# Moving statistics, the last addition of a convolution and unit orders in a fused graph-attention kernel

## The chip, the cores and the metric

One core of one Trainium2 chip runs the whole program; seven cores stand idle. The metric is the time of one execution in microseconds on the device. The engines of the core work side by side, each through its own queue in order: TensorE (PE in the profile; its weight loads are PEld), VectorE (DVE), ScalarE (ACT), GpSimd (POOL), and SyncE (SP), which issues the DMAs here. An instruction starts when what it waits for on other engines is done and everything ahead of it in its own queue has been issued.

## What is computed

Two layers for each of 32 batches of a 512 x 512 block x, in float32. The adjacency matrix adj is 512 x 512, of zeros and ones, shared by all batches.

```python
def attention(x, adj, Wq, bq, Wk, bk, Wv, bv):        # 8 heads of 64
    q, k, v = x @ Wq + bq, x @ Wk + bk, x @ Wv + bv   # split into heads
    scores = q @ k.T / sqrt(64) + where(adj == 0, -1e9, 0)
    return softmax(scores) @ v

def convolution(x, adj, W, b):
    return (adj @ x) @ W + b

x = layernorm(x + attention(x, adj, ...))     # first normalisation, "which" 0
x = layernorm(x + convolution(x, adj, W1, b1))  # second, "which" 1
```

## The kernel before

The fast path, `fast_kernel`, is followed by a general one that runs only when a check on the data fails (here it does not run). A batch's rows x lie in `X[b]` as four blocks of 128 rows (index c). A product of 512 x 512 x 512 is made by Strassen's scheme in Winograd's form: seven products of 256 x 256 x 256 (`FACTORS`, in the order 1, 5, 6, 7, 2, 3, 4), each of eight matmul records of 256 columns in the profile (L367), whose results VectorE, ScalarE and GpSimd add up. The left factors need three or four sums of blocks, which GpSimd makes (`combine_rows`, L329 to L331, and `sum_rows`, L357); the factors of q, k and v come from x transposed (`turn_squares`, L351).

Names for what follows, each with its lines:

- `project` (L367, evicted in L389 to L402): product i of q, k or v.
- `scores(b, g)` (L563 to L567): eight heads are taken in two groups g of four, each of two pairs hp. Sixteen score tiles of 128 x 512 go through eight PSUM banks (`bank`, a ring of 8, shared by all results of TensorE). VectorE empties each bank while masking it (L565), and ScalarE makes exponentials (L567) in the tiles `e`, of which there are 8. GpSimd adds the exponentials of a pair over the four blocks (`add_exponentials`, L578, into `es`).
- `attend` (L587): values times exponentials; the result is copied by ScalarE to `attT` (L591), of which there are two tiles. It also allots the tile `SQUARES`, one of the `e` tiles, for the fold.
- `fold_squares` (L598, L600): VectorE transposes and sums `es` of a pair; `add_up` (L608 to L613) finishes the softmax's sums and inverts them.
- `residual` (L619 to L624): TensorE turns `attT` over, VectorE multiplies by the inverse and adds to `X[b]`. After the last pair of a batch it issues the four `statistics` of the first normalisation (L429, L430: mean and variance of one block).
- `norm` (L433 to L445): a square root on ScalarE, its inverse and the shift on VectorE, four normalisations on ScalarE. `survey` gives the four statistics of the second normalisation.
- `split_high`, `split_low` (L455, L459, L460): x as a sum of two parts that the fast matmul format holds exactly; GpSimd adds the convolution's bias b1 to x after. `aggregate` (L486 to L492): adj times x, quarter d at a time.
- `convolve(b, i)` (L525 to L539): product i of the convolution. Its results go straight into the quarters x11, x12, x21, x22 of `X[b]`; a helper tile `MIX` collects the parts that several quarters share. Product 6 adds to MIX, and GpSimd adds MIX to x12; product 7 adds to MIX again, and GpSimd adds MIX to x22 and x21 (L537). Products 3 and 4 are then added to x12 and x21 by VectorE (L539).
- `look_for_low_half` (L306 to L309), once for each block of adj: does the fast format hold it exactly? ScalarE makes a copy, VectorE compares it (into a tile `attT`) and counts.

The order is written out by hand. `units_of(b)` makes the list of units that fill TensorE's time between the attentions of batch b: projections of batch b + 1, the split, aggregation and convolution of batch b - 1, the transposes of batch b + 2 and the normalisations. `behind[k]` is what is issued behind the k-th of the first 16 projection units. `weighed` gives each unit a weight (0.5 for a project or convolve, 0.55 for an aggregate, none for most), and `work_until(part)` issues units until that part of the group's weight is done. For each group the loop issues: two `attend`, the two folds, the next group's `scores`, `add_up`, units up to 0.85 (group 0) or 0.6 (group 1; 1.0 in the last batch but one, B - 2), the residuals, the rest of the units. `release()` issues the `add_exponentials` of the second pair, held back until a projection i = 7 has been issued (until any convolve in the last batch).

In the steady loop a batch therefore runs: attend(b, 0), folds, scores(b, 1), q, k and the first of v of batch b + 1 with the residual of group 0 among them; attend(b, 1), folds, scores(b + 1, 0), the rest of v, aggregation of b - 1, residual of group 1, statistics, convolution of b - 1. The last batch, t = B - 1 = 31, has no projections left; its list `units` holds the low halves of batch 30 (`lows`), the convolution of batch 29 (`older`), the aggregation of batch 30 (`gathered`) and the survey. After the loop come the convolution of batch 30, batch 31's normalisation by rows (`split_rows`, L500, L501; `aggregate_rows`, L513 to L523), its convolution, and a last normalisation by half blocks (`half_statistics`, L793).

## Time and profile before

| what | us |
|---|---|
| median of 3 runs | 2858.62 |
| lowest, highest | 2857.77, 2861.34 |
| profiled execution, span | 2858.2 |
| TensorE busy | 2820.5 |
| VectorE busy | 2086.4 |
| GpSimd busy | 1746.2 |
| ScalarE busy | 1146.6 |
| steady batch, start to start (1025.22 to 1113.04) | 87.82 |
| of which TensorE busy | 87.74 |

Busy time of an engine is the time in which the profile shows an instruction on it; ends of matmuls are modelled, so a wait between two matmuls of a pipelined run can be hidden in it. Times in the timelines are microseconds from the span's start. An entry in square brackets at the end of a timeline line is the time for which that engine stood idle before the instruction, and who ended it. The chain of waits is followed back from the last instruction to what released each step. A matmul of the program appears as two records or more, so counts of records are multiples of the program's.

### The profile page before, as it was taken

The numbers are of one execution on the slowest core, as the hardware profiler recorded it, in microseconds if no ns is written. First come the engines' busy times: TensorE is split into PE (matmuls) and PEld (weight loads), VectorE is DVE, ScalarE is ACT, GpSimd is POOL, SyncE is SP. The second block draws the span as 40 slices with busy tenths as digits, with TensorE's granted clock in tenths as the row PEclk, the third lists the DMA queues.
The fourth block names the chain that finished last, engine by engine and source line by source line (L and its number), as shares of the span: only waits on it lengthen the run. The fifth ranks groups of instructions, "written<-read, shape, count | busy, mean of one in ns | idle before, by whom it ended". The sixth has DMA issues, their size and how long they took to land.

```text
span 2858.2 us, 35612 instructions
## 1 busy us (share of the span) xinstructions
PE 2820.5 (99%) x13346; PEld 1983.1 (69%) x13346; DVE 2086.4 (73%) x3415; ACT 1146.6 (40%) x1550; POOL 1746.2 (61%) x1096
## 2 busy tenths in 40 slices
PE   8999999999999999999999999999999999999997
PEld 6676776766767767667677676676676766766765
DVE  6767777677776777777777767777677777777786
ACT  3344343343433443434434334343344342443443
POOL 4565665665756656656566656575665665665763
PEclk9999999999999999999999999999999999999998
DMA  5001111111101111011111111110111111111001
GB/s 154 12 8 41 45 30 30 41 34 45 45 16 45 34 41 45 16 45 34 41 45 35 25 42 33 45 45 15 45 34 41 45 24 36 36 39 45 30 16 45
DMA packets 302577, 108.81 MB, mean 38 GB/s; under 512 B 264256, under 2 KB 268352, under 8 KB 302400
## 3 DMA queue, kind: packets, MB, share of 16 engines
q1 hardware_dynamic: 302400, 106.47, 14.6%
q8 instruction: 108, 1.77, 0.3%
q14 instruction: 69, 0.57, 0.1%
HBM read 72.88 MB, written 33.55 MB: 37 GB/s over the span
## 4 chain that ended last, share of the span: by engine, by line
PE 96%; DVE 2%; POOL 1%; SPq 0%; issue 0%; ACT 0%; DMA 0%; DVEq 0%; ACTq 0%; POOLq 0%
PE bank L367 53%; PE bank L563 17%; PE bank L587 15%; PE bank L486 8%; PE bank L619 2%; PE bank L608 0%; POOL es L578 0%; DVE bnst L429 0%; SPq L253 0%; DMA xin<-in_x_dram 0%; DVE e L598 0%; POOL xs L460 0%; DVE bank L622 0%; POOL xs L537 0%; DVE part L600 0%
## 5 line engine op out<-in xcount | busy, mean ns | idle before, releaser
L565 DVE SCALAR_TENSOR_TENSOR e<-gap,bank 128x512 f32<-128x512 uint8 x1024 | 617.4, 678 | 65.0 <-PE bank L563 65.0
L578 POOL TENSOR_TENSOR es<-e 128x1024 f32<-128x1024 f32 x128 | 316.2, 2470 | 530.5 <-ACT e L567 530.5
L578 POOL TENSOR_TENSOR es<-es,e 128x1024 f32<-128x1024 f32 x256 | 618.7, 2417 | 20.1
L567 ACT ACTIVATE e<-e 128x1024 f32<-128x1024 f32 x512 | 524.2, 1052 | 130.8 <-DVE e L565 103.0
L591 ACT ACTIVATE attT<-bank 128x512 f32<-128x512 f32 x128 | 76.4, 598 | 1046.7 <-PE bank L587 1046.7
L563 PE MATMUL bank<-q,k 64*128 64x512 f32 x2048 | 488.4, 603 | 2.4 <-ACT attT L591 2.4
L587 PE MATMUL bank<-e,v 128*64 128x512 f32 x2048 | 453.8, 595 | 1.9 <-DVE v L402 1.9
L367 PE MATMUL bank<-wv,xT 128*128 128x256 f32 x1792 | 411.5, 381 | 3.1 <-DVE q L402 3.1
L563 PEld LDWEIGHTS bank<-q,k 64*128 64x128 f32 x2048 | 223.7, 186 | 265.6 <-issue 161.2
L367 PE MATMUL bank<-xT,wk 128*128 128x256 f32 x1792 | 404.0, 380 | 0.7 <-DVE wk L317 0.7
L367 PE MATMUL bank<-xT,wq 128*128 128x256 f32 x1792 | 401.0, 381 | 2.5 <-DVE wq L317 1.8
L367 PE MATMUL bank<-w,yT 128*128 128x256 f32 x1792 | 394.0, 380 | 1.6 <-DVE yT L518 1.6
L367 PEld LDWEIGHTS bank<-xT,wk 128*128 128x128 f32 x1792 | 341.1, 190 | 47.6 <-PE bank L367 1.1
L367 PEld LDWEIGHTS bank<-w,yT 128*128 128x128 f32 x1792 | 339.2, 191 | 47.2 <-DVE yT L518 2.0
L367 PEld LDWEIGHTS bank<-xT,wq 128*128 128x128 f32 x1792 | 337.7, 190 | 49.2 <-POOL xT L331 1.8
L367 PEld LDWEIGHTS bank<-wv,xT 128*128 128x128 f32 x1792 | 335.3, 190 | 49.3 <-issue 3.4
L587 PEld LDWEIGHTS bank<-e,v 128*64 128x64 f32 x2048 | 141.6, 137 | 278.8 <-issue 268.2
L537 POOL TENSOR_TENSOR xs<-xs,mix 128x512 f32<-128x512 f32 x93 | 117.6, 1279 | 204.2 <-DVE mix L535 204.2
L460 POOL TENSOR_TENSOR xs<-xs,b_r 128x512 f32<-128x512 f32 x124 | 157.2, 1278 | 114.4 <-DVE low L459 114.4
L402 DVE TENSOR_TENSOR q<-bank,q 128x512 f32<-128x512 f32 x96 | 66.4, 691 | 183.0 <-PE bank L367 157.2
L444 ACT ACTIVATE xs<-xs,shift,rstd 128x512 f32<-128x512 f32 x248 | 184.8, 811 | 29.8 <-DVE shift L439 29.8
L489 ACT ACTIVATE yT<-bank 128x512 f32<-128x512 f32 x124 | 74.3, 599 | 294.9 <-PE bank L486 294.9
(115 smaller groups left out, 3016.7 us busy)
## 6 DMA issues: line engine op xcount, KB each, us to landing
xin<-in_x_dram SPq DMA_DIRECT2D x496, 64.0 KB, 2.3
xs<-in_x_dram SPq DMA_DIRECT2D x31, 1024.0 KB, 5.1
out_dram<-xs SPq DMA_DIRECT2D x31, 1024.0 KB, 4.3
xin<-in_x_dram SPq DMA_DIRECT2D x4, 256.0 KB, 3.6
wq<-in_L_gnn_Wq_dram SPq DMA_DIRECT2D x2, 512.0 KB, 6.5
wk<-in_L_gnn_Wk_dram SPq DMA_DIRECT2D x2, 512.0 KB, 8.2
yT<-in_adj_dram SPq DMA_DIRECT2D x1, 1024.0 KB, 7.8
wv<-in_L_gnn_Wv_dram SPq DMA_DIRECT2D x2, 512.0 KB, 8.8
```

Of the source, the lines that this page charges most:

```text
L367: nc.tensor.matmul(pm[:, r, :], left[:, d, r * P:(r + 1) * P], right[:, d, :], start=(d == 0), stop=(d == 1))
L444: nc.scalar.activation(row, row, AF.Identity, bias=SHIFT[t][:, slot:slot + 1], scale=RSTD[t][:, slot:slot + 1])
L460: nc.gpsimd.tensor_add(cols, cols, b1_r[:, None, d * P:(d + 1) * P].to_broadcast([P, NB, P]))
L486: nc.tensor.matmul(pm.rearrange("p a n -> p (a n)"), part, adjT[:, n % NB, :], start=(n == 0), stop=(n == 2 * NB - 1))
L489: nc.scalar.activation(yt[:, d // 2:d // 2 + 3:2, d % 2, :], pm, AF.Copy)
L537: nc.gpsimd.tensor_add(block, block, MIX[b])
L563: nc.tensor.matmul(ps[s], keys[:, j * P:(j + 1) * P], queries, start=True, stop=True)
L565: nc.vector.scalar_tensor_tensor(e[:, s, :], gap[:, j, :], NEG * root, ps[s], op0=ALU.mult, op1=ALU.add)
L567: nc.scalar.activation(e, e, AF.Exp, scale=1.0 / root)
L578: nc.gpsimd.tensor_add(ES[b, hp], ES[b, hp] if j > 1 else E[b, hp, 0], E[b, hp, j])
L587: nc.tensor.matmul(po[s * HD:(s + 1) * HD, :], values, e[:, s, :], start=(j == 0), stop=(j == NB - 1))
L591: nc.scalar.activation(AT[b, hp], po, AF.Copy)
```

## The change

It has these parts:

1. In `convolve`, for all batches but the last, GpSimd adds MIX to x22 only behind product 7; it adds MIX to x21 after VectorE has added product 4 to x21 (a new line behind L539). In the last batch the order of the two is x21, x22 in place of x22, x21. The sums of the next factors (`turned[4:]`, that is `sum_rows`) are issued behind the seventh product of the convolution in place of the fifth.
2. The four statistics of the first normalisation are no longer issued by `residual`, but as units `fresh` among the q projections of the next batch (two each behind the fourth and fifth projection; all four behind the first in batch 1). Batch 30 keeps them in `residual`. The square root and inverse, made for both normalisations at once before (`both`, eight columns), become two of four columns each.
3. `look_for_low_half` moves in batch 0 from behind the projections of q and k to between those of v, two before and two after the residual.
4. In batch 30 `work_until` stops at 0.6 in place of 1.0 ahead of the residual of group 1.
5. In batch 31 two of the low halves of batch 30 are issued between the folds of group 0, and the last group's two folds are issued among the units (`last`), their results in a tile `v` in place of an `e` tile. `release()` is called before the second of these.
6. At the end, the survey of batch 30 is issued whole behind the first product of batch 31's convolution, not half of it before the aggregation; the half statistics of blocks 0 and 1 are taken behind product 3 alone, those of blocks 2 and 3 behind product 4.

```diff
@@ -533,10 +533,13 @@
             nc.scalar.activation(MIX[b], pm, AF.Copy)
         if i in (6, 7):
             nc.vector.tensor_add(MIX[b], pm, MIX[b])
-            for block in (x12,) if i == 6 else (x22, x21):
+            for block in (x12,) if i == 6 else (x21, x22) if b == B - 1 else (x22,):
                 nc.gpsimd.tensor_add(block, block, MIX[b])
         for block in {1: (x11,), 5: (x12, x22), 2: (x11,), 3: (x12,), 4: (x21,)}.get(i, ()):
             nc.vector.tensor_add(block, pm, block)
+        if i == 4 and b < B - 1:
+
+            nc.gpsimd.tensor_add(x21, x21, MIX[b])
 
     def aggregation(b):
 
@@ -586,7 +589,8 @@
                 values = V[b][hp // 2][:, j, h * HD:(h + 1) * HD]
                 nc.tensor.matmul(po[s * HD:(s + 1) * HD, :], values, e[:, s, :],
                                  start=(j == 0), stop=(j == NB - 1))
-        SQUARES[b, hp] = work.tile([P, 2, N], FP, name="e", bufs=8)
+        if (b, hp // PAIRS) != (B - 1, HP // PAIRS - 1):
+            SQUARES[b, hp] = work.tile([P, 2, N], FP, name="e", bufs=8)
         AT[b, hp] = work.tile([P, N], FP, name="attT")
         nc.scalar.activation(AT[b, hp], po, AF.Copy)
 
@@ -594,7 +598,11 @@
 
         if hp % PAIRS == 0:
             PART[b, hp // PAIRS] = work.tile([P, GROUP, N // SQ], FP, name="part", bufs=1)
-        square = SQUARES.pop((b, hp))
+        if (b, hp // PAIRS) == (B - 1, HP // PAIRS - 1):
+
+            square = work.tile([P, 2, N], FP, name="v", bufs=3)
+        else:
+            square = SQUARES.pop((b, hp))
         nc.vector.transpose(square.rearrange("p s n -> p (s n)"), ES.pop((b, hp)).rearrange("p s n -> p (s n)"))
         heads = slice(2 * (hp % PAIRS), 2 * (hp % PAIRS) + 2)
         nc.vector.tensor_reduce(PART[b, hp // PAIRS][:, heads, :], square.rearrange("p s (j f) -> p s j f", f=SQ),
@@ -622,7 +630,7 @@
         nc.vector.tensor_mul(pt, pt, inverse[:, :, :, None].to_broadcast([P, NB, 2, HD]))
         cols = X[b][:, :, hp * P:(hp + 1) * P]
         nc.vector.tensor_add(cols, pt.rearrange("p c s d -> p c (s d)"), cols)
-        if hp == HP - 1 and b < B - 1:
+        if hp == HP - 1 and b == B - 2:
             for c in range(NB):
                 statistics(b, 0, c)
 
@@ -689,16 +697,18 @@
 
             older = convolution(b - 2)
             lows = [(split_low, b - 1, d) for d in range(DB - 1)]
-            units = weighed(lows[:2] + older[:3] + lows[2:] + splits[3:] + older[3:5] + older[5:] + gathered + seen)
+            last = folds(b, 1)
+            units = weighed(older[:3] + last[:1] + lows[2:] + splits[3:] + older[3:] + gathered + last[1:] + seen)
             return units, [sum(w for _, w in units)] * 2
 
+        fresh = [(statistics, b - 1, 0, c) for c in range(NB)] if young else []
         if old:
-            both = [[(f, b - 1, slice(0, 2 * NB))] for f in (square_root, invert_root)]
-            behind = [seen[:2], seen[2:]] + both + [old[2:4], old[4:] + ready] + [[u] for u in young[2:]]
+            behind = [seen[:2], seen[2:], old[:2], old[2:4] + fresh[:2], old[4:] + ready + fresh[2:]] + [
+                [u] for u in young]
         else:
-            behind = [ready] + [[u] for u in young]
+            behind = [ready + fresh] + [[u] for u in young]
         if b == 0:
-            behind = [[]] + [[(sum_weights, w1, n)] for n in range(4)] + [[(look_for_low_half, c)] for c in range(NB)]
+            behind = [[]] + [[(sum_weights, w1, n)] for n in range(4)]
         behind += [[] for _ in range(11 - len(behind))] + [splits[:1], [], splits[1:2]]
         behind += [[] for _ in range(16 - len(behind))]
         units = []
@@ -706,13 +716,14 @@
             units += [unit] + behind[k]
         first = sum(w for _, w in weighed(units))
         values = made[16:]
-        units += values[:3] + gathered[:1] + splits[2:3] + gathered[1:2] + values[3:] + splits[3:]
+        looked = [(look_for_low_half, c) for c in range(NB)] if b == 0 else []
+        units += values[:3] + looked[:2] + gathered[:1] + splits[2:3] + gathered[1:2] + values[3:] + looked[2:] + splits[3:]
         if b == B - 2 > 0:
             units += [(load, B - 1)]
         units += gathered[2:3] + turned[:1] + gathered[3:]
         convolved = convolution(b - 1) if b < B - 2 else []
         for k in range(7):
-            units += convolved[k:k + 1] + (turned[k + 1:k + 2] if k < 3 else turned[4:] if k == 4 else [])
+            units += convolved[k:k + 1] + (turned[k + 1:k + 2] if k < 3 else turned[4:] if k == 6 else [])
         units = weighed(units)
         return units, [first, sum(w for _, w in units)]
 
@@ -733,6 +744,8 @@
             begin = ends[g - 1] if g else 0.0
             while units and (units[0][1] == 0 or done < begin + (ends[g] - begin) * part - 0.3):
                 unit, w = units.pop(0)
+                if unit[0] == fold_squares and unit[2] % PAIRS:
+                    release()
                 run([unit])
                 done += w
                 if unit[0] == (project if b < B - 1 else convolve):
@@ -741,17 +754,17 @@
 
         for hp in range(g * PAIRS, (g + 1) * PAIRS):
             attend(b, hp)
-        folded = folds(b, g)
         if i == len(groups) - 1:
-            run(folded)
             add_up(b, g)
             break
-        run(folded[:1] + flips(1) + folded[1:] if i == 0 else folded)
+        between = flips(1) if i == 0 else [(split_low, b - 1, d) for d in range(2)] if i == len(groups) - 2 else []
+        folded = folds(b, g)
+        run(folded[:1] + between + folded[1:])
         later = scores(*groups[i + 1])
         add_up(b, g)
         if g == 0 and b + 2 < B:
             load_squares(b + 2)
-        work_until((0.6 if b != B - 2 else 1.0) if g else 0.85)
+        work_until(0.6 if g else 0.85)
         for hp in range(g * PAIRS, (g + 1) * PAIRS):
             residual(b, hp)
         work_until(1.0)
@@ -780,7 +793,6 @@
     run(rest[3 + NB:])
     for c in range(NB):
         add_bias(t, c)
-    run(seen[:2])
     aggregate_rows(t)
 
 
@@ -793,14 +805,14 @@
         nc.vector.bn_stats(halves[c][:, s, :], X[t][:, c, s * half:(s + 1) * half])
 
     old = norm(t, 1)
-    beside = {1: seen[2:], 2: old[:2], 5: old[2:3], 6: old[3:5], 7: old[5:]}
+    beside = {1: seen, 2: old[:2], 5: old[2:3], 6: old[3:5], 7: old[5:]}
     for unit in last:
         run([unit] + beside.get(unit[2], []))
         if unit[2] == 2:
             well = judge()
         if unit[2] == 7 and t > 0:
             store(t - 1)
-        for c, s in {2: ((0, 0), (1, 0)), 3: ((2, 1), (3, 1), (0, 1), (1, 1)), 4: ((2, 0), (3, 0))}.get(unit[2], ()):
+        for c, s in {2: ((0, 0), (1, 0)), 3: ((0, 1), (1, 1)), 4: ((2, 1), (3, 1), (2, 0), (3, 0))}.get(unit[2], ()):
             half_statistics(c, s)
             if (c < 2) == (s == 1):
                 if t + 1 not in STAT:
```

## The prediction

> **What bounds the kernel now.** First the page: busy time, then the chain of waits by engine.
>
> ```profile
> PE 2820.5 (99%) x13346; PEld 1983.1 (69%) x13346; DVE 2086.4 (73%) x3415; ACT 1146.6 (40%) x1550; POOL 1746.2 (61%) x1096
> ...
> PE 96%; DVE 2%; POOL 1%; SPq 0%; issue 0%; ACT 0%; DMA 0%; DVEq 0%; ACTq 0%; POOLq 0%
> ```
>
> TensorE sets the time, and the 1% in which it is idle (37.7 us) is small. So I looked inside its busy time: TensorE's timeline, for pieces of one kind that last longer than their like. Columns: start us, length us, engine, line, operation, tiles, shape, count, then the wait.
>
> ```profile
> 99.12 2.68 PE L367 MATMUL bank<-wv,xT 128*128 128x256 f32 x8 [3.15 <-DVE q L402]
> ...
> 139.30 7.69 PE L563 MATMUL bank<-q,k 64*128 64x512 f32 x32
> ...
> 1060.94 7.21 PE L563 MATMUL bank<-q,k 64*128 64x512 f32 x32
> ...
> 1085.64 12.25 PE L367 MATMUL bank<-w,yT 128*128 128x256 f32 x56
> 1097.83 7.09 PE L587 MATMUL bank<-e,v 128*64 128x512 f32 x32
> 1104.84 8.07 PE L563 MATMUL bank<-q,k 64*128 64x512 f32 x32
> ...
> 2766.48 5.56 PE L563 MATMUL bank<-q,k 64*128 64x512 f32 x20 [2.36 <-ACT attT L591]
> ...
> 2793.91 3.41 PE L486 MATMUL bank<-adjT,k 128*128 128x512 f32 x8 [2.93 <-DVE mix L535]
> ...
> 2808.63 0.31 PE L608 MATMUL bank<-part,fold 128*32 128x16 f32 x8 [4.29 <-DVE part L600]
> ...
> 2834.27 11.92 PE L367 MATMUL bank<-w,yT 128*128 128x256 f32 x54 [1.65 <-DVE yT L518]
> ```
>
> Scores (L563) take 7.21 us after a projection, but 8.07 after the convolution and attend (1085.64, 1097.83): 0.86 us more, with no wait shown. The chain of waits has that longer piece (8.00 or 8.01) once in each of 29 batches, every 87.8 us from 226.8 to 2685.6. VectorE's timeline shows why:
>
> ```profile
> 95.64 0.69 DVE L308 TENSOR_TENSOR attT<-yT,high 128x512 f32<-128x512 f32 x1 [13.03 <-PE bank L619]
> ...
> 140.95 9.64 DVE L565 SCALAR_TENSOR_TENSOR e<-gap,bank 128x512 f32<-128x512 uint8 x16
> ...
> 1062.10 9.65 DVE L565 SCALAR_TENSOR_TENSOR e<-gap,bank 128x512 f32<-128x512 uint8 x16 [2.15 <-PE bank L563]
> ...
> 1098.14 0.69 DVE L535 TENSOR_TENSOR mix<-bank,mix 128x512 f32<-128x512 f32 x1 [1.38 <-POOL xs L537]
> 1098.75 0.68 DVE L539 TENSOR_TENSOR xs<-bank,xs 128x512 f32<-128x512 f32 x1
> 1101.46 0.69 DVE L539 TENSOR_TENSOR xs<-bank,xs 128x512 f32<-128x512 f32 x1 [2.03 <-POOL xs L537]
> ...
> 1106.88 9.64 DVE L565 SCALAR_TENSOR_TENSOR e<-gap,bank 128x512 f32<-128x512 uint8 x16
> ```
>
> L565 empties the score banks. Where VectorE waits for it (1062.10, 1.16 us after the scores began at 1060.94) TensorE loses nothing. Where L565 comes behind a backlog TensorE runs out of banks: begun 2.04 us after the scores, the loss is 0.86; 1.65 us after (140.95 against 139.30), 7.69 - 7.21 = 0.48. So loss = lateness - 1.17, which I use throughout.
>
> **What the skill says.** "Trainium Kernel Development and Optimization", Performance Expectations, calls matmul busy time a bad metric, as matmuls are pipelined: the hidden 0.86 us agrees. "TensorE: Matmul & The Clock Gate", Part 1: The HAM clock gate, says that about 3.4 us of idleness halves the clock until some 3.4 us of work are done: after the wait of 3.15 us eight records take 2.68 us in place of 1.89; after 2.36 us none slows. "GPSIMD Engine Reference", 8. Key points: it shares SBUF interfaces with VectorE operations of two SBUF inputs; L459, such an operation, takes 680 ns at least, 906 in the median and 2775 at most, ending about where a GpSimd instruction ends.
>
> **The change part by part**, against the profiled span, 2858.2 us (timed: 2857.8 to 2861.3, median 2858.6).
>
> *Loop.* Four statistics pairs (L429, L430; 1088.72 to 1091.93 = 3.21 us) leave VectorE ahead of the convolution's additions, and the addition of block x21 no longer waits 2.03 us for GpSimd, which adds MIX after it. Replayed with the row lengths: VectorE is done with the residual at 1088.7; additions 1 and 2 and their two transposes end at 1091.2, 5 at 1092.4, the third transpose at 1093.0, mix 6 at 1093.6, GpSimd's x12 1.27 us later at 1094.95, mix 7 at 1095.7. From there the products set the pace (12.25/7 = 1.73 each): addition 3 at 1096.7, 4 at 1098.5, in place of 1102.1. The folds need the first score tile free (1.15 us into attend, as at 1142.86 - 1141.73): 1099.0 + 4.8 = 1103.8. L565 then waits for its bank, so lateness 1.16, loss 0: 29 x 0.86 = **24.9 us**. Either half suffices: without the wait alone the folds end at 1104.8; without the statistics alone x21's wait ends at 1098.3. A larger gain isn't there, as TensorE then runs without a gap.
>
> The statistics go to the next batch, between evictions of q. There VectorE idles 0.37 + 4.56 + 1.03 us up to 1128.9, more than 3.21. Behind them stand ScalarE's second square root, an eviction of k and the normalisation: root at about 1124.8, high halves done near 1130, before 1130.7; price 0. The square root is split, but both share one table load: 0.3 us on an idle ScalarE. GpSimd's x21 now ends at 1099.8, its four row sums, moved behind it, at 1104.9 (before 1106.5). On SyncE the store and load keep their order and come no later.
>
> *Start.* L308 waited 13.03 us for attend's tile, holding q's evictions, and TensorE stood 3.15 us: 95.70 to 106.15 = 10.4 us for work of 5.2 (three times 1.73). Moving the four L308/L309 pairs gives 5.2 us. But they now stand at 126.6 to 138, ahead of the folds: 4 x 1.31 = 5.3 us in place of 3.2 of statistics, on a VectorE that is late, beside running GpSimd. Two wait some 2.4 us for its additions. The first pairs move v's last evictions to 133.5 to 135.9; L565 begins at 145.4, and scores end at 145.4 - 1.17 + 7.14 = 151.4, before 146.9. Without contention 149.1, with a halved clock 153. Net: 5.2 - 4.5 = **+0.7** (-1.5 to +3).
>
> *Tail.* In batch 30 the residual goes ahead of the last v products, so statistics of 3.2 us precede v's evictions and the fourth low half: VectorE 2746.3 to 2749.1 to 2752.3 to 2753.5, low at 2754.2 to 2755.4. The fourth aggregation waits 2 to 3 us, a new loss. Two low halves go between the folds, and L565 begins at 2766.9 (2766.0): scores end 0.9 later. In return 3.4 us of low halves are gone behind it, x21 doesn't wait (2.02), and each last fold stands earlier: mix 7 ends at 2792.0 (2793.85), so the waits of 2.93 and 4.29 go, with their half clock (3.41 for 1.89; 1.97 for 1.04; 13.83 for 12.25). Attend starts at 2793.9 (2797.25); adding up at 2801.0 (2808.6); seven products end at 2814.6 (2824.1): 9.5 us. At the end two statistics no longer precede the copy L518, but all four follow convolution 1: the 1.65 us wait goes and 0.3 remains on VectorE. Taking x21 first and block statistics of rows 0 and 1 before x22 saves about 1.0. Sum **10.8** (4 to 13).
>
> Sum: 24.9 + 0.7 + 10.8 = 36.4; 2858.2 - 36.4 = 2821.8, **2822** for the timed median.
>
> **Rivals.**
> - *The tail gives little*: the new wait at the fourth aggregation exceeds 3.4 us, halves the clock and spreads. For: 2 to 3 us come from GpSimd's boundaries, unknown to a microsecond. Against: later slack absorbs it. Gain 25 + 2: 2831.
> - *Half the loop's gain*: the additions wait for products and GpSimd more than I replayed, L565 late by 1.6 us. Against: 1.6 us between 1103.8 and the first bank. 2858.2 - 12.5 - 11 = 2835.
> - *Edges better than computed*: no contention at the start, tail 13: 2817.
> - *Slower*: the next batch's row sums stand behind GpSimd's x21 and so behind VectorE's addition 4; product 5 of q, their first reader, starts near 1113.9. If addition 4 ended later than 1113.9 - 6.4 = 1107.5, each us costs 29; from 1108.8 the sum is a loss, at 1109.5 some 2880. Against: I place it at 1098.5.
> - *It doesn't do what it says*: x21 could still wait for x22, its neighbour. The built program has that addition wait for TensorE alone; and x22 would be done at 1097.0 anyway. No change: 2858.
>
> **Chances.** Forecast 0.66 (own range 2817 to 2827), tail 0.13, half 0.07, better 0.09, slower 0.03, no change 0.02. 0.2% (5.7 us) is about what a measurement tells from none. Faster 0.95, same 0.02, slower 0.03. Range 2814 to 2834: the forecast, the better case and most of the tail's.
>
> **What would show it.** Right: all L563 pieces of the loop 7.21; batches of 86.95 in place of 87.82; L539 with no GpSimd wait; no wait at 95.7, scores near 140 longer than 7.69; TensorE not idle 2.9 and 4.3 us near the end, but 2 to 3 us in L486 before attend. Wrong: a piece near 8.0 in the loop, or a new wait for q's banks or row sums.

## The result, and the profile after

| | us |
|---|---|
| before, median of 4 runs beside it (lowest, highest) | 2859.65 (2857.77, 2861.34) |
| after, median of 4 runs (lowest, highest) | 2826.01 (2825.79, 2826.57) |
| ratio, 95% interval | 0.9883, 0.9866 to 0.9900 |
| predicted, range | 2822, 2814 to 2834 |
| profiled execution, before and after | 2858.2 and 2824.3 |

The change makes the kernel 1.2% faster: 33.9 us between the two profiled executions, where the prediction's sum was 36.4. The likeliest case of the prediction came true, in the steady loop almost to the digit. One term of its sum, the tail, was too large by 2.3 us.

Lines shift a little in the changed kernel: scores are L566 (before L563), the emptying of their banks L568 (L565), attend L590 (L587), the folds L606 and L608 (L598 and L600), adding up L616 (L608), the turning over of the residual L627 (L619). Up to L539 nothing shifts.

The page of the changed kernel, busy time and the chain of waits by engine:

```profile
PE 2794.3 (99%) x13346; PEld 1960.4 (69%) x13346; DVE 2119.7 (75%) x3473; ACT 1155.0 (41%) x1579; POOL 1747.6 (62%) x1096
...
PE 97%; DVE 2%; SPq 0%; issue 0%; ACT 0%; DMA 0%; POOL 0%; DVEq 0%; ACTq 0%
```

TensorE still sets the time. It has the same 13346 matmuls and is "busy" for 26 us less: the gain lay inside busy time, as the prediction read it. VectorE is busy for 33 us more, and that costs nothing: the shift L439 runs 65 times in place of 36 and takes 28.1 us in all in place of 6.0, the reciprocal L438 5 us more.

TensorE's timeline of the changed kernel, at the start, in one steady batch and near the end (start, length, operation, tiles, count, then the wait):

```profile
129.26 5.37 PE L590 MATMUL bank<-e,v 128*64 128x512 f32 x24 [1.74 <-DVE v L402]
134.56 3.70 PE L566 MATMUL bank<-q,k 64*128 64x512 f32 x16
141.06 5.31 PE L566 MATMUL bank<-q,k 64*128 64x512 f32 x16 [2.79 <-DVE e L568]
...
1095.65 7.21 PE L566 MATMUL bank<-q,k 64*128 64x512 f32 x32
...
2729.64 1.18 PE L486 MATMUL bank<-adjT,low 128*128 128x512 f32 x4 [2.88 <-DVE low L459]
2730.65 1.74 PE L486 MATMUL bank<-adjT,high 128*128 128x512 f32 x4
2732.32 8.03 PE L590 MATMUL bank<-e,v 128*64 128x512 f32 x32
2740.28 9.11 PE L566 MATMUL bank<-q,k 64*128 64x512 f32 x32
...
2799.61 11.92 PE L367 MATMUL bank<-w,yT 128*128 128x256 f32 x54 [0.45 <-DVE yT L518]
```

Scores after the convolution and attend now take 7.21 us (1095.65) in place of 8.07. All 57 score pieces from the second of batch 2 to the second of batch 30 last 7.21. At the start and near the end scores are long (134.56 to 146.37; 9.11), and a wait of 2.88 us stands at L486 ahead of attend, with half-clock work behind it: 1.74 for 1.09 and 8.03 for 7.09.

VectorE's timeline of the changed kernel shows what is different in the loop, at 1096.82, and at both ends:

```profile
140.33 9.64 DVE L568 SCALAR_TENSOR_TENSOR e<-gap,bank 128x512 f32<-128x512 uint8 x16
...
1088.75 0.69 DVE L539 TENSOR_TENSOR xs<-bank,xs 128x512 f32<-128x512 f32 x1 [1.03 <-PE bank L367]
...
1096.82 9.65 DVE L568 SCALAR_TENSOR_TENSOR e<-gap,bank 128x512 f32<-128x512 uint8 x16 [2.15 <-PE bank L566]
...
2743.35 9.64 DVE L568 SCALAR_TENSOR_TENSOR e<-gap,bank 128x512 f32<-128x512 uint8 x16
```

In the loop L568 waits 2.15 us for the first score bank and begins 1.17 us behind the scores, where it began 2.04 us behind them before. The addition to x21 (1088.75) waits for its product, no longer for GpSimd. At both ends L568 has no wait in front of it: there it is late, by 5.77 us (140.33 against 134.56) and by 3.07 us (2743.35 against 2740.28). The prediction's law (loss = lateness - 1.17 us) holds there too: the scores take 11.81 us, 4.60 more than 7.21, where 5.77 - 1.17 is 4.60; and 9.11 us, 1.90 more, where 3.07 - 1.17 is 1.90.

To see where the time went, I cut each span at starts that TensorE's timeline gives: first scores, scores of batch 2 group 0, scores of batch 31 group 0, end of the last scores, first L513, end of the span.

| stretch, us | before | after | gain | predicted |
|---|---|---|---|---|
| to the first scores | 41.64 | 42.10 | -0.46 | 0 |
| start: to batch 2 | 141.19 | 140.11 | 1.08 | 0.7 |
| loop: to batch 31 | 2546.64 | 2521.87 | 24.77 | 24.9 |
| tail, to the end of the last scores | 42.57 | 45.32 | -2.75 | -0.9 |
| tail, on to L513 | 52.10 | 41.02 | 11.08 | 10.4 |
| tail, on to the end | 34.11 | 33.89 | 0.22 | 1.3 |

The last three are the tail: 8.55 us in place of 10.8. The first line is work ahead of anything that the change touches, and over all kernels below it lies between 40.6 and 42.7, so I take it as scatter.

### The profile page after: what moved, and what is told of

The parts are those of the page before. It is cut to its first block, busy times and chain, and to the rows that moved or that the text cites. A ratio compares the mean times of both kernels' runs of the same rounds, so it can differ in the third digit from the quotient of the medians.

```text
span 2824.3 us, 35602 instructions
## 1 busy us (share of the span) xinstructions
PE 2794.3 (99%) x13346; PEld 1960.4 (69%) x13346; DVE 2119.7 (75%) x3473; ACT 1155.0 (41%) x1579; POOL 1747.6 (62%) x1096
## 4 chain that ended last, share of the span: by engine, by line
PE 97%; DVE 2%; SPq 0%; issue 0%; ACT 0%; DMA 0%; POOL 0%; DVEq 0%; ACTq 0%
PE bank L367 54%; PE bank L566 16%; PE bank L590 15%; PE bank L486 8%; PE bank L627 2%; PE bank L616 0%; SPq L253 0%; DMA xin<-in_x_dram 0%; DVE bnst L429 0%; DVE attT L308 0%; DVE low L459 0%; DVE e L606 0%; DVE xT L539 0%; PE bank L513 0%; DVE v L402 0%
## 5 line engine op out<-in xcount | busy, mean ns | idle before, releaser
L568 DVE SCALAR_TENSOR_TENSOR e<-gap,bank 128x512 f32<-128x512 uint8 x1024 | 617.8, 680 | 129.0 <-PE bank L566 129.0
L581 POOL TENSOR_TENSOR es<-e 128x1024 f32<-128x1024 f32 x128 | 316.4, 2472 | 545.1 <-ACT e L570 545.1
L581 POOL TENSOR_TENSOR es<-es,e 128x1024 f32<-128x1024 f32 x256 | 618.3, 2415 | 20.1
L566 PE MATMUL bank<-q,k 64*128 64x512 f32 x2048 | 465.4, 599 | 2.9 <-DVE e L568 2.8
L590 PE MATMUL bank<-e,v 128*64 128x512 f32 x2048 | 454.7, 596 | 1.7 <-DVE v L402 1.7
L566 PEld LDWEIGHTS bank<-q,k 64*128 64x128 f32 x2048 | 203.8, 186 | 262.9 <-issue 204.4
L367 PEld LDWEIGHTS bank<-w,yT 128*128 128x128 f32 x1792 | 338.0, 190 | 45.6 <-DVE yT L518 0.9
L590 PEld LDWEIGHTS bank<-e,v 128*64 128x64 f32 x2048 | 141.8, 137 | 279.8 <-issue 269.2
L489 ACT ACTIVATE yT<-bank 128x512 f32<-128x512 f32 x124 | 74.3, 599 | 294.6 <-PE bank L486 294.6
L459 DVE TENSOR_TENSOR low<-xs,high 128x512 fp32r<-128x512 f32 x122 | 126.4, 1037 | 70.9 <-ACT high L455 70.9
L606 DVE STREAM_TRANSPOSE e<-es 128x1024 f32<-128x1024 f32 x126 | 156.2, 1240 | 17.9 <-PE bank L590 17.8
```

The source lines that it names most:

```text
L367: nc.tensor.matmul(pm[:, r, :], left[:, d, r * P:(r + 1) * P], right[:, d, :], start=(d == 0), stop=(d == 1))
L459: nc.vector.tensor_sub(LOW[b, d], cols, HIGH[b, d].bitcast(FP))
L566: nc.tensor.matmul(ps[s], keys[:, j * P:(j + 1) * P], queries, start=True, stop=True)
L568: nc.vector.scalar_tensor_tensor(e[:, s, :], gap[:, j, :], NEG * root, ps[s], op0=ALU.mult, op1=ALU.add)
L581: nc.gpsimd.tensor_add(ES[b, hp], ES[b, hp] if j > 1 else E[b, hp, 0], E[b, hp, j])
L590: nc.tensor.matmul(po[s * HD:(s + 1) * HD, :], values, e[:, s, :], start=(j == 0), stop=(j == NB - 1))
```

## The experiments

All times are medians; each run had runs of the kernel before beside it, with medians of 2858.7 to 2860.6. The changed kernel was not run again beside them, so a difference of 1 to 2 us from it cannot be read from medians alone, and I also give the stretches of the table above from the profiled execution of each.

| kernel | median | start | loop | to end of last scores | L513 to the end |
|---|---|---|---|---|---|
| before | 2859.65 | 141.19 | 2546.64 | 42.57 | 34.11 |
| after | 2826.01 | 140.11 | 2521.87 | 45.32 | 33.89 |
| x21_alone | 2834.00 | 141.19 | 2521.59 | 43.53 | 34.08 |
| stats_alone | 2831.98 | 138.69 | 2521.87 | 42.61 | 34.23 |
| two_more | 2825.49 | 140.54 | 2521.42 | 44.67 | 34.19 |
| four_more | 2840.74 | 141.13 | 2536.23 | 44.65 | 33.87 |
| look_back | 2826.02 | 140.04 | 2521.98 | 45.56 | 33.56 |
| look_tile | 2820.39 | 133.60 | 2521.94 | 44.69 | 34.40 |
| stats30_late | 2824.33 | 140.53 | 2521.76 | 42.72 | 33.79 |
| whole_stage | 2828.17 | 141.11 | 2521.95 | 46.62 | 34.18 |
| low_first | 2825.23 | 140.79 | 2521.08 | 43.51 | 34.00 |
| low_earlier | 2813.15 | 140.95 | 2512.40 | 41.83 | 33.87 |
| old_end | 2827.91 | 140.11 | 2521.88 | 45.57 | 35.42 |
| best | 2805.66 | 133.62 | 2512.84 | 40.48 | 34.10 |

Kernels with the same code in a stretch show how firm such a number is. The loop repeats within 0.5 us, the start of the changed kernel lies between 140.1 and 141.1, and the stretch to the end of the last scores between 44.7 and 45.6.

The spread of the last two comes from the clock granted to TensorE. Eight of these runs have the start of the changed kernel, with a wait of 2.79 us in the late scores (141.06 in the changed kernel). In six of them the clock was 0.50 for 3.41 us behind that wait, and the start took 140.53 to 141.13; in the changed kernel itself and in old_end it was not halved, and the start took 140.11. Near the end the wait of 2.9 us at L486 was followed by half clock in the changed kernel, look_back and old_end (45.32 to 45.57), and not in two_more, four_more and look_tile (44.65 to 44.69). So up to 1.0 us at the start and 0.6 to 0.9 near the end are luck, whatever the order of the work.

### Each half of the loop's change alone

x21_alone: the kernel before, with

```diff
-            for block in (x12,) if i == 6 else (x22, x21):
+            for block in (x12,) if i == 6 else (x22,) if b < B - 3 else (x22, x21):
...
             nc.vector.tensor_add(block, pm, block)
+        if i == 4 and b < B - 3:
+            nc.gpsimd.tensor_add(x21, x21, MIX[b])
...
-            ... (turned[k + 1:k + 2] if k < 3 else turned[4:] if k == 4 else [])
+            ... (turned[k + 1:k + 2] if k < 3 else turned[4:] if k == 6 else [])
```

> The kernel before with one half of the change, in the convolutions of the loop alone: GpSimd's addition to block x21 behind VectorE's, and the four row sums behind it. The statistics stay where they were, both ends stay as before. Theory (either half is enough, since scores lose only what L565 is later than 1.17 us behind their start): the folds end at about 1104.8 of the profile of before, 1.2 us ahead of the first score bank; every score piece of the loop lasts 7.21 us, 29 x 0.86 = 24.9 us go, and the time is about 2834.5 us. Rival (VectorE's work adds up, each half is worth its share of the 5.2 us that leave VectorE, 2.03 of them here): about 10 us go, some 2849 us.

stats_alone: the kernel before, with the changed kernel's `fresh` and `behind`, and

```diff
-        if hp == HP - 1 and b < B - 1:
+        if hp == HP - 1 and b == B - 2:
```

> The kernel before with the other half: the first half's statistics of batches 0 to 29 go to the next batch, between the evictions of q, with the split of the second square root. GpSimd adds MIX to x21 ahead of VectorE as before, and both ends stay as before but for batch 0's statistics, which leave the start. Theory (either half is enough): every score piece of the loop lasts 7.21 us, 24.9 us go; at the start the statistics of batch 0 no longer hold v's evictions, which is worth up to 2 us more: 2832 to 2834.5 us. Rival (halves add up, 3.21 of the 5.2 us here): some 15 us go, 2843 us. In both, the addition to x21 still waits about 2 us for GpSimd.

Measured: 2834.00 us (ratio 0.9908, 0.9891 to 0.9924) and 2831.98 us (0.9900, 0.9884 to 0.9917). VectorE's timeline in one steady batch, first of x21_alone:

```profile
1096.74 9.65 DVE L567 SCALAR_TENSOR_TENSOR e<-gap,bank 128x512 f32<-128x512 uint8 x16 [1.17 <-PE bank L565]
```

then of stats_alone:

```profile
1086.63 0.69 DVE L539 TENSOR_TENSOR xs<-bank,xs 128x512 f32<-128x512 f32 x1 [1.36 <-POOL xs L537]
...
1094.38 9.65 DVE L565 SCALAR_TENSOR_TENSOR e<-gap,bank 128x512 f32<-128x512 uint8 x16 [2.15 <-PE bank L563]
```

In both the bank is the last thing waited for. In stats_alone the addition to x21 still waits 1.36 us for GpSimd, and that costs nothing. The loop gives 25.05 us with the one half, 24.77 with the other, and 24.77 with both: the two gains don't add. The rival, in which each half brings its share of VectorE's time, is out. What the second half buys is slack only: 2.15 us of waiting in place of 1.17. stats_alone's start is 2.50 us shorter than before, a little more than I had allowed (2).

### How much lateness is free

two_more and four_more: the changed kernel with 2 or 4 pairs of statistics, whose results nobody uses, behind the units of the convolution of batches 1 to 29 (4 in the second):

```diff
+    def repeat(b, c):
+        st = work.tile([P, nc.vector.BN_STATS_DIM], FP, name="bnst")
+        nc.vector.bn_stats(st, X[b][:, c % NB, :])
+        nc.vector.bn_aggr(extra, st)
...
+        units += [(repeat, b, c) for c in range(2)] if 0 < b < B - 2 else []
         units = weighed(units)
```

> The changed kernel with work put on VectorE that computes nothing needed: two more pairs of statistics (L429, L430) in each of the batches 1 to 29, behind the convolution's last addition and ahead of the folds, 1.6 us by the rows of before. Theory (lateness of L568 behind the scores decides): the folds come 1.3 us later, since 0.33 us of idle time lies ahead of them, and end some 0.8 us ahead of the first score bank, so L568 still waits for its bank: 0 us, within 0.1%. Rival (VectorE sets the time together with TensorE, so that each of its us counts): 29 x 1.6 = 46 us slower.

> As two_more, with four pairs, 3.2 us. Theory: the folds come 2.9 us later and end 0.7 us behind the moment at which the first score bank is there, so L568 begins 1.8 to 1.9 us behind the scores; loss = lateness - 1.17 = about 0.7 us per batch, score pieces of 7.9 us in place of 7.21, 29 x 0.7 = 20 us slower than the changed kernel (2846 us). Rival (each us of VectorE counts): 93 us slower. Together with two_more it tells whether there is a threshold and what slope lies behind it.

Measured: 2825.49 us, 0.5 from the changed kernel, and 2840.74 us, 14.7 slower. TensorE's timeline of four_more:

```profile
1100.70 7.72 PE L572 MATMUL bank<-q,k 64*128 64x512 f32 x32
```

and VectorE's, the last of the added work and the emptying of the banks (L574 here), between them the folds:

```profile
1097.50 0.18 DVE L436 BATCH_NORM_AGGREGATE extra<-bnst 128x2 f32<-128x6 f32 x1
...
1102.39 9.64 DVE L574 SCALAR_TENSOR_TENSOR e<-gap,bank 128x512 f32<-128x512 uint8 x16
```

Lateness 1102.39 - 1100.70 = 1.69; by the prediction's law the loss is 1.69 - 1.17 = 0.52, and the piece is longer by 7.72 - 7.21 = 0.51. 29 x 0.51 = 14.8; the times show 14.7, the loop's stretch 14.4. My expectation was 20, as I had placed L568 0.1 to 0.2 us later in each batch than it came. The first 1.6 us are free, of the next 1.6 us a third is paid. This is the firmest result of the study: a threshold, and behind it one for one.

### The start: the comparison of adj

look_back: the changed kernel with the four L308/L309 pairs where they were before:

```diff
-            behind = [[]] + [[(sum_weights, w1, n)] for n in range(4)]
+            behind = [[]] + [[(sum_weights, w1, n)] for n in range(4)] + [[(look_for_low_half, c)] for c in range(NB)]
...
-        looked = [(look_for_low_half, c) for c in range(NB)] if b == 0 else []
+        looked = []
```

> The changed kernel with the part of the start undone: the four L308/L309 pairs go back behind the projections of q and k, where they stood before. Theory of the prediction, sharpened by stats_alone, whose start is the same (from the first scores to those of batch 2, group 0: 138.7 us there, 140.1 in the changed kernel): L308 waits for attend's tile again and TensorE stands for 3.15 us, but VectorE is no longer late for v's evictions and for L568 near 140; net about 1.4 us faster, some 2824.5 us. Rival (moving them is a gain of 5 us, what comes later has other causes): 5 us slower, 2831 us.

look_tile: the same, and in `look_for_low_half`

```diff
-        cut = work.tile([P, N], FP, name="attT")
+        cut = work.tile([P, N], FP, name="cut", tag="low", bufs=2)
```

> As look_back, and L308 writes to a tile of another name, low, which is free then, so that it waits for no attend. Theory (the wait is for the tile, and the place early on VectorE is good): neither the 3.15 us of TensorE nor the lateness near 140 is there; 5 us less than look_back, 6.5 less than the changed kernel, some 2819.5 us. Rival (without the wait the four pairs hold the evictions of q by their own 5.3 us, or GpSimd's addition holds them): at most 2 us less than look_back, some 2823 us.

Measured: 2826.02 us, nothing, where 1.4 us less was expected; and 2820.39 us, 5.6 less than both, where 5 less than look_back and 6.5 less than the changed kernel were expected. TensorE's timeline of look_back:

```profile
98.73 3.75 PE L367 MATMUL bank<-wv,xT 128*128 128x256 f32 x8 [3.15 <-DVE q L402]
102.27 4.90 PE L367 MATMUL bank<-xT,wk 128*128 128x256 f32 x16
107.11 7.09 PE L590 MATMUL bank<-e,v 128*64 128x512 f32 x32
```

The wait is the one of before, 3.15 us; but the 24 records behind it take 8.38 us (98.73 to 107.11), where they took 7.03 before (99.12 to 106.15) and in stats_alone, and 5.27 with no wait (96.26 to 101.53 in the changed kernel). The same wait therefore cost 1.8 us of half clock twice and 3.1 us once, and that is what my 1.4 us went into. The granted clock was 0.50 for 3.41 us before (from 100.22) and in stats_alone (from 99.02), but for 6.83 us in look_back (from 98.04). The Trainium skill, "TensorE: Matmul & The Clock Gate", Part 1: The HAM clock gate, says that the window over which activity is judged is free-running and takes no notice of a kernel's start. That the price of a wait therefore depends on where the wait falls in a window is my inference; the traces agree, as in each of them all changes of the clock lie whole multiples of 3.41 us apart. As a move, this part of the change is worth nothing that shows within 1 us: the wait at 95 is exchanged for lateness at 134 (a wait of 1.74 for v, then scores of 11.8 us for 7.2).

VectorE's timeline of look_tile:

```profile
83.63 2.16 DVE L308 TENSOR_TENSOR cut<-yT,high 128x512 f32<-128x512 f32 x1 [1.83 <-ACT high L306]
...
86.42 2.12 DVE L308 TENSOR_TENSOR cut<-yT,high 128x512 f32<-128x512 f32 x1
...
132.57 9.65 DVE L568 SCALAR_TENSOR_TENSOR e<-gap,bank 128x512 f32<-128x512 uint8 x16 [0.20 <-PE bank L566]
```

L308 waits 1.83 us, for its own copy, in place of 13.03 us for attend's tile. Two of them last 2.1 us beside GpSimd, but they now do so while VectorE has time. Both losses are gone, and the start is 6.5 us shorter. The wait was for a name.

### The tail: what makes L568 late

stats30_late: the changed kernel, batch 30's statistics behind v's last evictions and the fourth low half:

```diff
-        if hp == HP - 1 and b == B - 2:
-            for c in range(NB):
-                statistics(b, 0, c)
...
+        if b == B - 2 > 0:
+            units += [(statistics, b, 0, c) for c in range(NB)]
```

> The changed kernel with batch 30's statistics behind v's last evictions and the fourth low half, in place of directly behind the residual. Theory: the wait of 2.88 us at L486 comes from the 3.2 us of statistics ahead of the low half; without it attend starts about 3.4 us earlier at full clock, the square root (behind both the statistics and ScalarE's copy L489) comes some 2 to 3 us earlier and L568 with it: 2 to 3.5 us faster, some 2823 us. Rival (the square root follows the statistics, which now end 2.5 us later, so L568 is no earlier and the scores end where they did): 0.

whole_stage: the changed kernel with

```diff
-        work_until(0.6 if g else 0.85)
+        work_until((0.6 if b != B - 2 else 1.0) if g else 0.85)
```

> The changed kernel with the residual of batch 30 behind all work of that stage, as before (the 1.0 in work_until). Theory: the L486 wait goes and attend starts some 3.4 us earlier, but residual, statistics, square root and normalisation follow one another, and set L568: scores end where they did, within 1 us (2825 to 2827 us). Rival (the wait at L486 itself is the cost): 3.4 us faster, 2822.5 us. Less than 1 us from the changed kernel cannot be told by times; the trace tells it then by the end of the scores near 2749.

Measured: 2824.33 us, 1.7 less, where 2 to 3.5 were expected; and 2828.17 us, 2.2 more, where at most 1 was expected. (One more execution of whole_stage took 7879.73 us, for a reason that no kept trace shows; with it the median is 2828.79.) To the end of the last scores stats30_late takes 42.72 us, 2.6 less than the changed kernel, and whole_stage 46.62, 1.3 more. ScalarE's timeline of the changed kernel shows what the prediction did not follow, that the root stands behind the last aggregation's copy:

```profile
2732.43 0.60 ACT L489 ACTIVATE yT<-bank 128x512 f32<-128x512 f32 x1 [5.04 <-PE bank L486]
2733.04 1.28 ACT L433 ACT_TABLE_LOAD   x1
2734.34 0.30 ACT L433 ACTIVATE rstd<-stat,eps 128x4 f32<-128x4 f32 x1
2736.11 2.93 ACT L444 ACTIVATE xs<-xs,shift,rstd 128x512 f32<-128x512 f32 x4 [1.47 <-DVE shift L439]
```

and VectorE's, from there to L568 at 2743.35:

```profile
2734.88 1.19 DVE L439 SCALAR_TENSOR_TENSOR shift<-stat,rstd 128x4 f32<-128x4 f32 x1
...
2739.73 1.29 DVE L459 TENSOR_TENSOR low<-xs,high 128x512 fp32r<-128x512 f32 x2 [1.25 <-ACT high L455]
```

The wait at L486 delays its copy L489, that delays the square root, and root, shift, normalisation, high halves, low halves and the second fold follow each other up to L568, which decides when the scores end. In stats30_late ScalarE reads:

```profile
2730.58 0.60 ACT L489 ACTIVATE yT<-bank 128x512 f32<-128x512 f32 x1 [3.17 <-PE bank L486]
...
2732.49 0.30 ACT L433 ACTIVATE rstd<-stat,eps 128x4 f32<-128x4 f32 x1
```

TensorE of stats30_late:

```profile
2728.44 1.17 PE L486 MATMUL bank<-adjT,low 128*128 128x512 f32 x4 [1.67 <-DVE low L459]
2729.45 1.10 PE L486 MATMUL bank<-adjT,high 128*128 128x512 f32 x4
```

and VectorE of stats30_late:

```profile
2725.64 2.66 DVE L459 TENSOR_TENSOR low<-xs,high 128x512 fp32r<-128x512 f32 x1
...
2733.04 0.47 DVE L439 SCALAR_TENSOR_TENSOR shift<-stat,rstd 128x4 f32<-128x4 f32 x1
```

The root is 1.85 us earlier, L568 at 2740.78 is 2.57 us earlier, the scores end 2.6 us earlier. The rival (no gain) is out. I had expected the wait at L486 to go; but the low half, now ahead of the statistics, takes 2.66 us beside a GpSimd instruction, and a wait of 1.67 us is left. Of the 2.57 us, 1.2 are the shorter wait, 0.64 the full clock behind it (1.10 for 1.74 at L486), which is luck, and 0.72 the shift L439, which takes 0.47 us in place of 1.19.

In whole_stage there is no wait at L486 and attend starts at 2730.34 - 2705.54 = 24.80 us behind the scores of group 0 in place of 28.25, but the statistics end at 2736.6, and the root comes at 2736.66. VectorE's timeline of whole_stage goes on:

```profile
2741.02 1.29 DVE L459 TENSOR_TENSOR low<-xs,high 128x512 fp32r<-128x512 f32 x2 [1.25 <-ACT high L455]
...
2744.64 9.64 DVE L568 SCALAR_TENSOR_TENSOR e<-gap,bank 128x512 f32<-128x512 uint8 x16
```

and TensorE's:

```profile
2742.56 1.61 PE L566 MATMUL bank<-q,k 64*128 64x512 f32 x4 [2.35 <-ACT attT L595]
2745.37 6.79 PE L566 MATMUL bank<-q,k 64*128 64x512 f32 x16 [1.20 <-DVE e L568]
```

L568 begins 2744.64 - 2705.54 = 39.10 us behind the scores of group 0, against 2743.35 - 2704.07 = 39.28 in the changed kernel: where it did, as the theory said, so the rival (3.4 us faster) is out. That the scores still end 1.3 us later comes from the clock: it was 0.50 for 6.83 us from 2744.20, behind the waits of 2.35 and 1.20 us, and the last sixteen records take 6.79 us, where they take 5.30 in look_tile. In stats30_late L568 begins 36.68 us behind those scores, 2.4 earlier than in whole_stage, so stopping at 0.6 ahead of the residual pays once the fourth low half does not stand behind the statistics.

Against the kernel before, something else makes L568 late. There VectorE's timeline reads:

```profile
2766.01 9.64 DVE L565 SCALAR_TENSOR_TENSOR e<-gap,bank 128x512 f32<-128x512 uint8 x16
```

Counted from the start of the scores of group 0, at 2729.47, the root (2760.57) came after 31.1 us there, as in whole_stage, and L565 after 36.54. In whole_stage L568 comes 2.56 us later than that, and 2.54 of it are the two low halves between the folds: they wait 1.25 us for ScalarE's high halves and last 1.29. In the changed kernel the root comes 0.84 us earlier than before, the low halves cost 2.54, and the shift L439 takes 1.03 more: 2.73 of the 2.74 us by which L568 is later.

### The low half and GpSimd

low_first and low_earlier: the changed kernel, the fourth low half ahead of the last, or of both last, of v's evictions:

```diff
-        units += ... + values[3:] + looked[2:] + splits[3:]
+        units += ... + values[3:4] + splits[3:] + values[4:] + looked[2:]      # low_first
+        units += ... + splits[3:] + values[3:] + looked[2:]                    # low_earlier
```

> The changed kernel with the fourth low half (L459) one step earlier on VectorE, ahead of the last of v's evictions in place of behind it. In the changed kernel each batch's fourth aggregation starts 0.25 us late for it (the pair of aggregations takes 4.2 us, against 3.9 where nothing waits), about 0.3 us x 29. Theory (L459 has two SBUF inputs and ends 0.55 us after a GpSimd instruction ends, here at 1072.96, wherever in that instruction it begins): the low half begins 1.6 us earlier and ends at 1073.5 as before; 0 us, within 0.1% of the changed kernel. Rival (VectorE's order sets when it ends): 8 to 9 us faster, 2817 us.

> As low_first, two steps earlier, ahead of both of v's evictions: the high half is there at 1069.4 and the GpSimd instruction then running ends at 1070.5. Theory (end of the GpSimd instruction plus 0.55 us): the low half ends at 1071.05, ahead of the aggregation's need at 1073.4, and 0.3 us x 29 = 8 to 9 us go; in batch 30 it also stands ahead of residual and statistics, so the wait at L486 near the end goes or turns into one for v's evictions, 0 to 2 us more: 2815 to 2818 us. Rival (the 0.3 us comes from something else in TensorE's pair of aggregations, or v's evictions, now 1 us later, hold a bank): 0 in the loop, 2824 to 2826 us.

Measured: 2825.23 us, 0.8 less than the changed kernel, and 2813.15 us, 12.9 less (ratio 0.9839, 0.9822 to 0.9855). VectorE and GpSimd in the same batch; low_first, VectorE:

```profile
1071.88 2.79 DVE L459 TENSOR_TENSOR low<-xs,high 128x512 fp32r<-128x512 f32 x1
```

low_first, GpSimd:

```profile
1071.76 2.37 POOL L581 TENSOR_TENSOR es<-es,e 128x1024 f32<-128x1024 f32 x1
```

low_earlier, VectorE:

```profile
1065.99 1.62 DVE L459 TENSOR_TENSOR low<-xs,high 128x512 fp32r<-128x512 f32 x1 [1.14 <-ACT high L455]
```

low_earlier, GpSimd:

```profile
1064.26 2.81 POOL L581 TENSOR_TENSOR es<-e 128x1024 f32<-128x1024 f32 x1
```

GpSimd's instruction ends at 1074.13 and the low half at 1074.67; in low_earlier at 1067.07 and 1067.61. The difference is 0.54 us both times, whether the low half has begun 2.25 or 1.08 us ahead of that end. Placed 1.6 us earlier it ends when it ended, and the loop gains 0.8 us, 0.03 in each batch; placed two steps earlier it falls behind the GpSimd instruction before, and the loop is 9.47 us shorter, 0.33 in each of 29 batches. In the tail the wait at L486 is gone, and the stretch to the end of the last scores is 3.5 us shorter. The Trainium skill, "SBUF — State Buffer", Terms, says that VectorE and GpSimd lock a shared pair of ports for a whole instruction and that the loser blocks fully. The trace agrees in each of the 63 low halves of the changed kernel that last over 0.8 us: they end 0.544 to 0.551 us behind the end of a GpSimd instruction.

### The orders at the very end

old_end: the changed kernel with

```diff
-            for block in (x12,) if i == 6 else (x21, x22) if b == B - 1 else (x22,):
+            for block in (x12,) if i == 6 else (x22, x21) if b == B - 1 else (x22,):
...
+    run(seen[:2])
     aggregate_rows(t)
...
-    beside = {1: seen, 2: old[:2], 5: old[2:3], 6: old[3:5], 7: old[5:]}
+    beside = {1: seen[2:], 2: old[:2], 5: old[2:3], 6: old[3:5], 7: old[5:]}
...
-        for c, s in {2: ((0, 0), (1, 0)), 3: ((0, 1), (1, 1)), 4: ((2, 1), (3, 1), (2, 0), (3, 0))}.get(unit[2], ()):
+        for c, s in {2: ((0, 0), (1, 0)), 3: ((2, 1), (3, 1), (0, 1), (1, 1)), 4: ((2, 0), (3, 0))}.get(unit[2], ()):
```

> The changed kernel with the orders of the very end as before: two statistics ahead of the copy L518, x22 ahead of x21, and the half statistics of blocks 2 and 3 ahead of those of rows 0 and 1. The prediction's step: 0.3 us at the copy and 1.0 us at the last convolution, so 1.3 us slower, 2827.3 us. Rival, from the two traces (from the start of L513 to the end the change gained only 0.2 us): 0.2 us slower, not to be told. The trace decides: from the start of L513 to the end of the span 33.9 us in the changed kernel.

Measured: 2827.91 us, 1.9 more; from L513 to the end 35.42 us, 1.5 more. By the number alone, the step undone is worth what the prediction gave it (1.3), and the rival, which I had formed from the two traces (0.2), misses. TensorE's timeline of old_end shows why the two traces say less:

```profile
2800.78 13.61 PE L367 MATMUL bank<-w,yT 128*128 128x256 f32 x54 [2.04 <-DVE yT L518]
```

In the kernel before, the same order cost a wait of 1.65 us, and the 54 records behind it took 11.92 us. Here it costs 2.04 us, and they take 13.61: the clock granted is 0.50 for 3.41 us from 2801.50, which the wait of 1.65 us had not brought. In these two traces the old order costs more in the new kernel than in the old one, and 1.69 us of that are the clock, so that the agreement with 1.3 is partly luck. From the end of these records to the end of the span the three need 12.1 us (before), 12.8 (after) and 11.0 (old_end), so what TensorE loses ahead is partly taken back by VectorE's work behind it, and of the 1.0 us that the prediction expected there nothing is seen. Which of the three orders brings how much, and what they are worth at full clock, the run doesn't separate.

### A version that beats both

best: the changed kernel with low_earlier's and look_tile's edits, and near the end

```diff
-        run(folded[:1] + between + folded[1:])
+        run(folded[:1] + between + folded[1:] if i == 0 else folded + between)
```

> The changed kernel with what the runs point to: the fourth low half ahead of both of v's evictions (low_earlier), the four L308/L309 pairs behind the projections with a tile of another name (look_tile), and near the end both folds ahead of the two low halves that stood between them, which wait 1.25 us for ScalarE. Theory (these are three different places in time, so the gains add up): low_earlier's 2813.2 less 7.3 us at the start (133.6 us from the first scores to batch 2 in look_tile, 141.0 in low_earlier) less 1.2 us near the end = 2804.7 us. Rival (the start's gain is taken back at the next wait for a buffer, or the end's by the low halves that the convolution needs): 2808 to 2813 us.

Measured: 2805.66 us (2804.98 to 2807.08), ratio to before 0.9816 (0.9803 to 0.9829). The start takes 133.62 us and the loop 2512.84, as in the runs that these edits come from; to the end of the last scores it is 40.48, 1.35 less than in low_earlier. The rival, that something is taken back, is out. TensorE's waits in best (waited for, by whom: total us, times, longest):

```profile
PE bank L340 <- DMA xin<-in_x_dram: 3.8, 1, 3.8
PE bank L367 <- DVE wk L317: 0.7, 1, 0.7
PE bank L367 <- DMA wq<-in_L_gnn_Wq_dram: 0.6, 1, 0.6
PE bank L367 <- DVE yT L518: 0.5, 1, 0.5
PE bank L513 <- DVE low L501: 0.3, 1, 0.3
```

and in the changed kernel:

```profile
...
PE bank L486 <- DVE low L459: 3.3, 2, 2.9
PE bank L566 <- DVE e L568: 2.8, 1, 2.8
PE bank L590 <- DVE v L402: 1.7, 1, 1.7
...
```

These three are gone; no entry of best belongs to the loop.

## Why the prediction was right, and where it was not

- **The loop, 24.9 us: right.** It came to 24.77. The law (loss = lateness - 1.17 us) and the threshold stood the test of added work, which it sized within 0.01 us per batch once the lateness was read. "Either half suffices" was shown by the two halves alone. The wait in front of L568 shows where the unneeded rest of the gain lies: VectorE's new idle time. One sum was wrong on the safe side: by the prediction's own numbers the margin from 1103.8 to the first bank (1104.84 + 1.16 = 1106.0) is 2.2 us, not 1.6, and L568 waited 2.15.
- **No cost of the moved statistics, square root and row sums: right.** All score pieces are 7.21, and the loop's TensorE shows no new wait but one of 0.40 us, at L486 in a single batch.
- **The start, +0.7 us: right in sum** (1.08; but in six of eight traces with this start the clock was halved in the late scores, and there the gain is 0.06 to 0.66). The lateness came as computed: L565 was placed at 145.4, less the 5.2 us gained ahead and with the 0.46 us of the first stretch 140.7, measured 140.33. That the move is worth nothing within 1 us is shown by its undoing.
- **The tail, 10.8 us: mechanism right, size wrong.** It was 8.5. The wait of 2 to 3 us at L486 came (2.88), and the waits of 2.93 and 4.29 us with their half clock went, as said. Three terms were mis-sized. "L565 begins at 2766.9, scores end 0.9 later" was 2.75 later. The prediction follows VectorE alone up to L568 and names nothing that holds it there: the two low halves between the folds wait for ScalarE (2.54 us with their work), the shift is slow beside GpSimd (1.03), and the square root queues behind the copy of the aggregation that I had just made late, so that it came only 0.84 us earlier. The other order of stats30_late takes 2.6 us of it back, 0.6 of them by the clock, and both folds ahead of the low halves another 1.35 (best against low_earlier). From there to L513 the gain was 11.08 for 10.4; no run undoes the moved folds and low halves (part 5) alone, so that this gain is theirs is read from the waits that are gone, and not shown by an undoing. "About 1.3 at the end" was 0.22 between the two traces, and 1.5 when undone.
- **Half clock behind the new wait: not foreseen in the forecast.** I had put it at waits over 3.4 us, and only in a rival, although the prediction's own lines showed it after 3.15 and 2.93 us. After 2.88 us the clock was halved; of the slower work, 0.65 us in L486 and 0.94 in L590, some 0.6 reached the end of the scores. In three other runs the same wait was not followed by half clock, so the miss holds a piece of bad luck.
- **The rivals.** "Slower", through the next batch's row sums, needed addition 4 behind 1107.5. It ends at 1089.44, 6.2 us ahead of the scores; on the scale of before, where these start at 1104.84, that is 1098.6, and I had placed it at 1098.5. No wait for row sums appears. "The tail gives little" was half there: the wait did halve the clock and did delay L568, but it cost 2 us, not the 9 that it would have taken.

## What to carry to other kernels

Where an engine feeds another through a ring of banks, don't ask how busy it is, but how late it comes to the ring behind the first result; up to a threshold (1.17 us here) work on it is free, behind it each microsecond is paid once per pass, and two repairs of the same lateness don't add up. When work is moved, follow each queue to the next deadline (here from TensorE's aggregation through a copy on ScalarE to a square root and back to VectorE), since a wait that "later slack absorbs" may sit ahead of a queue that has none. And before moving an instruction that waits, look at what it waits for: twice here it was not the order but a tile's name or a GpSimd instruction's end.

## What the runs showed of the hardware that I had not expected

- A low half (L459, 128 x 512, two SBUF inputs) that begins while a GpSimd instruction runs and is held by it ends a fixed 0.54 to 0.55 us behind that one's end, and not earlier if begun earlier. Tiny operations seem to be hit too: L439, on 128 x 4 elements, took 0.16 us in whole_stage and 1.19 us in the changed kernel, where it ended (2736.07) with the GpSimd instruction that began at 2734.78 and lasted 1.27 us. In the loop of the changed kernel one L439 of each batch, 29 in all, took 0.73 us on average and ended 0.02 us behind an L581 of GpSimd each time; the 35 others took 0.16 to 0.18 us. GpSimd pays as well: L581 lasts 2.7 to 2.8 us where a low half that began ahead of it is still running in its first half microsecond, 2.37 otherwise.
- The length of a wait doesn't tell alone whether the clock is halved. It was after single waits of 2.04 us (old_end), 2.36 (x21_alone), 2.88 (after) and 2.93, 3.15 and 4.29 (before), and not after 2.36 (before), 2.79 (after), 2.90 (two_more) and 2.94 (stats_alone). What tells it better is the grid of 3.41 us on which the clock changes. I cut each of the fourteen traces, from the first scores to 20 us before the end, into windows of this grid and added up TensorE's idle time in each. Of the windows at full clock, all 18 with 1.95 us idle or more were followed by half clock, none with 1.40 or less, and 3 of the 21 between.
